# A chain of four layers on one core: the products of layers 1 and 2 in another order, both batches' high weight blocks first, then both batches' low ones

## The chip, the cores and the metric

The kernel runs on one core of a Trainium2 chip. TensorE multiplies, VectorE (DVE in the profile) and ScalarE (ACT) do elementwise work, GpSimd (POOL) folds and issues some transfers, SyncE (SP) issues most transfers. The metric is the time of one execution on the device in microseconds; lower is better. Times shown are of the slowest core, and there is only one.

## The reference, cut to what matters

`x` has 8 batches of 256 tokens by 1024 features. Four layers follow one another, each with a residual:

```python
x = x + L0(x)     # x W^T, plus a gated mixture of 8 rank-16 experts
x = x + L1(x)     # x W^T + b + coeff[b] * (x @ (2*mask[b] - 1))
x = x + L2(x)     # x @ weight[id[b]]^T
x = x + L3(x)     # (x @ B[id[b]]^T) @ A[id[b]]^T
```

In layer 1 the product's matrix is W^T plus a scaled mask of signs, another one for each batch; in layer 2 it is one of 8 weights, chosen for each batch by its id. So in layers 1 and 2 every batch has a 1024 by 1024 matrix of its own. Inputs are in float32.

## The kernel before, in words

**Precision by parts.** A float32 matrix is split into a high part ([...]`whi` for weights) and a low part (the rest, `wlo`). A product is high times high, plus high times low, plus low times high. Activations of layers 1 and 2 are kept in tiles `hl`, with the high and the low part of a batch's 256 tokens side by side, 512 columns. So a *unit*, which is one block m of 128 output features for one batch, takes eight wide products (a block of `whi` against 512 columns, one for each 128 input features k) and eight narrow ones (a block of `wlo` against the 256 high columns). Both kinds go into the same bank of PSUM; the evacuation adds its two halves. `two` writes these sixteen products: the loop at L529 with the wide ones at L531, the loop at L538 with the narrow ones at L540. Between the two loops it runs `mid`, pieces of other layers' work handed in by `main`; `early` comes after the second wide product. `late` stays empty.

**Batches and groups.** A pair q (0 to 3) is two batches, j = 0 and 1. Two pairs make a group g. Layer 0 is computed for a group at a time, in 16 slots s; then for each of its pairs come layer 1 and layer 2, each 16 units u, in the order m outside, j inside (in the last pair the last six units of layer 2 go by j outside). So even u is batch j = 0 of a block m and odd u is batch j = 1 of the same block.

**Joint units.** `main(n)` does one unit. In layer 1 for m < 7, and in layer 2 (in the last pair for u < 10), the two units of a block are *joint*: they share a PSUM tile of two banks (`ps`, two such tiles alternate), and both are evacuated at once after the odd one. The other units have a tile each.

**The order of each slot.** There is no scheduler: `unit_slot(n)` writes out what each engine does, and every engine keeps that order. It issues the load of the unit nine ahead, stores finished outputs, evacuates what the slots before have finished (ScalarE copies one half, VectorE adds the other: `c<-po` or `sum<-po`), casts the high part of the unit four ahead (`highs`, ScalarE, L288), adds W to a scaled mask (`merge_add`, VectorE; the W tile has two buffers), subtracts for the low parts (`lows`, VectorE, `wlo`), and then calls `main`. Low parts are made up to unit `f + LO_AHEAD + 1 - lag`, with LO_AHEAD = 3 and a lag of 1, more in the five slots of `LAGS` (L31) around the step from layer 1 to layer 2. There are five buffers of `whi` and four of `wlo`, and nine of raw weights or masks. A transfer that fills a raw buffer waits until the subtraction has read what was in it.

**Work put between.** In layer 2 of q = 1 and q = 3 the middle pieces are layer 3 of the pair before: `proj_pair` at u = 1 (L442), `rank_pair` at u = 3 (L453, L454), and at u = 5, 6, 7 and 8 `fill(2)`, which twice calls `finish`: two narrow products (L470) into a PSUM bank of its own, and an addition of it to the output rows on VectorE (`c<-pf`). Of the two `finish` in a fill the first takes bank 2 and the second bank 3, each time, and there is one buffer of each. In q = 1 the router's products of the next group stand at u = 13 (L308) and transposes of their result at u = 14 (L319). In q = 3, u = 9 has projections of the last two batches (L489), and others follow from u = 13 on.

Of the kernel before, what the change touches and what calls it, by code (L numbers as in the profile page):

```python
# [17 lines left out]
T = 256  # L18
N = 2 * T
K = 8  # L20
# [14 lines left out]
def kernel(ctx: ExitStack, tc: tile.TileContext, x, lang, coeff, ids,  # L35
# [28 lines left out]
    mm = nc.tensor.matmul  # L64
    copy = nc.scalar.copy

    def tt(o, a, b, op):
        nc.vector.tensor_tensor(o, a, b, op)  # L68
# [142 lines left out]
    def by_dma(q, m):  # L211
        return q % 2 == 0 and 2 * m < ADDED
# [20 lines left out]
    def fold_block(t, eng=None):  # L233

        (eng or nc.gpsimd).tensor_tensor(t, t, ident, ALU.add)  # L235
# [24 lines left out]
    def merge_add(n):  # L260
        _, q, m, j = items[n]
        s = f32(raws[n])
        if by_dma(q, m):
            fold_block(s[:, m, :])
            nc.gpsimd.dma_start(s, w1[m], accum_op=ALU.add)
            return
        if j == 0:
            fold_block(w1raw[q, m][:, m, :])
        tt(s, s, w1raw[q, m], ALU.add)
# [31 lines left out]
    def logits(p):  # L301


        g, j = p // 2, 1 - p % 2
        pl = bank(j, f"pl{p}")
        for k in range(K):
            c = 32 * (k % 4)
            mm(pl[c:c + 32, :], wrs[:, k, :], X[g][:, j, k, :], start=(k < 4), stop=(k >= 4))  # L308

        def leave():  # L310
            lgs[p] = gp.tile([P, N], F32, tag="lg", name=f"lg{p}", bufs=3)
            copy(lgs[p], pl)
        return leave

    def by_token(p):
        pts[p] = bank(1 - p % 2, f"pt{p}")
        lg = lgs.pop(p)
        for n in range(4):
            nc.tensor.transpose(pts[p][:, n * P:(n + 1) * P], lg[:, n * P:(n + 1) * P], ident)  # L319
# [114 lines left out]
    def proj_pair(q, n):  # L434


        pb = bank(n, f"pb{q}")
        for j in range(2):
            b = 2 * q + j
            for k in range(K):  # L440
                c = 32 * (k % 4)
                mm(pb[c:c + 32, j * T:(j + 1) * T], l3b[b][:, k, :], xts[b][:, k, :],  # L442
                   start=(k < 4), stop=(k >= 4))
        hi = gp.tile([P, N], FR, tag="lg", name=f"pbhi{q}", bufs=3)
        lo = gp.tile([P, N], FR, tag="lg", name=f"pblo{q}", bufs=3)
        copy(hi, pb)
        tt(lo, pb, f32(hi), ALU.subtract)
        prs[q] = hi, lo

    def rank_pair(q, n, banks):  # L450
        hi, lo = prs.pop(q)
        pr = bank(n, f"pr{q}")
        mm(pr[:96], sel3, hi, start=True, stop=False)  # L453
        mm(pr[:96], sel3, lo, start=False, stop=True)  # L454
        rt = l3p.tile([96, N], FR, tag="rt", name=f"rt{q}", bufs=1)
        copy(rt, pr[:96])
        tt(rt[32:64, :], pr[32:64, :], f32(rt[32:64, :]), ALU.subtract)
        for j in range(2):
            for m in range(0, K, 2):
                fillers.append(lambda b=2 * q + j, m=m, n=banks[m // 2 % 2]: finish(  # L460
                    b, m, rt[:, (b % 2) * T:(b % 2 + 1) * T], n))
# [14 lines left out]
    def fill(n=1):  # L476
        for _ in range(min(n, len(fillers))):
            fillers.pop(0)()
# [40 lines left out]
    def rank(b):  # L519
        sums.pop(b)()  # L520
        rt = third(b)
        for m in range(0, K, 2):
            fillers.append(lambda m=m: finish(b, m, rt, (0, 2)[m // 2 % 2]))


    def two(po, hi, lo, xhl, j, early=(), mid=(), late=()):


        for k in range(K):  # L529
            c = slice(k * P, (k + 1) * P)  # L530
            mm(po, hi[:, c], xhl[:, k, j].rearrange("p h t -> p (h t)"), start=(k == 0),  # L531
               stop=False)
            if k == 1:
                for f in early:
                    f()
        for f in mid:
            f()
        for k in range(K):  # L538
            c = slice(k * P, (k + 1) * P)
            mm(po[:, :T], lo[:, c], xhl[:, k, j, 0, :], start=False, stop=(k == K - 1))  # L540
        for f in late:
            f()

    def three(po, hi, lo, xhl, j):
        for k in range(K):
            c = slice(k * P, (k + 1) * P)
            for h in range(2):
                mm(po, hi[:, c], xhl[:, k, j, h, :], start=(k + h == 0), stop=False)  # L548
        for k in range(K):
            c = slice(k * P, (k + 1) * P)  # L550
            mm(po, lo[:, c], xhl[:, k, j, 0, :], start=False, stop=(k == K - 1))
# [45 lines left out]
    def link(*args, **kw):  # L597

        mm(*args, skip_group_check=True, **kw)  # L599
# [263 lines left out]

    pos_tile = {}

    def main(n):

        kind, q, m, j = slots[n]
        u = (pos[slots[n]]) % 16
        f = first[n]  # L870
        hi, lo = his.pop(f), los.pop(f)
        early, mid, late = [], [], []
        last = n == len(slots) - 1

        end = q == 3 and kind == "L2"
        joint = u < 10 if end else (m < K - 1 or kind == "L2")
        h = u % 2 if joint else 0
        if h == 0:
            pos_tile[0] = ps.tile([P, 2, N], F32, tag="mm", name=f"po{n}")
        po = pos_tile[0][:, h, :]  # L880
        xh = hls[kind, q]
        if kind == "L1":
            if u == 0:
                hls["L2", q] = hl_tile(GX[q // 2], f"hl2_{q}")
        else:
            if u == 0:
                i = 2 - 2 * (q % 2)
                xt2 = G[q // 2][:, i:i + 2].rearrange(
                    "p j a (b t) -> p j (a b) t", b=2)
                xts[q, 2] = xt2  # L890
                xts[2 * q], xts[2 * q + 1] = xt2[:, 0], xt2[:, 1]
            if q % 2:
                if u == 1:
                    mid = [lambda: proj_pair(q - 1, 2)]
                if u == 3:
                    mid = [lambda: rank_pair(q - 1, 3, (2, 3))]
                if 5 <= u < 9:
                    mid = [lambda: fill(2)]
            if q == 1:
                if u == 13:  # L900
                    mid = [lambda: [leave() for leave in [logits(p) for p in (2, 3)]]]
                if u == 14:
                    mid = [lambda: [by_token(p) for p in (2, 3)]]
            if q == 3:
                b = NB - 1
                if u == 9:
                    mid = [lambda: proj(b - 1, 0, 0), lambda: proj(b, 0, 1)]
                if u == 13:
                    mid = [lambda: proj(b - 1, 1, 0)]
                if u == 14:  # L910
                    early = [lambda: rank(b - 1)]
                    mid = [lambda: fill(2)]
        if last:

            po = po[:, :T]
            three(po, hi, lo, xh, j)
        else:
            two(po, hi, lo, xh, j, early=early, mid=mid, late=late)
        if joint and u % 2 == 0:
            return  # L920
        js = slice(0, 2) if joint else slice(j, j + 1)
        po = pos_tile[0] if joint else pos_tile[0][:, :1, :]
        if last:
            po = po[:, :, :T]
        if kind == "L1":
            x2 = hls["L2", q][:, m, js]
            done.append((po, b1_sb[:, m:m + 1], None, x2[:, :, 0, :], x2[:, :, 1, :]))
        else:
            done.append((po, None, xts[q, 2][:, js, m, :], None, None))
# [36 lines left out]
    def unit_slot(n):  # L966
        kind, q, m, j = slots[n]
        f = first[n]
        i = pos[slots[n]]
        g, ahead = divmod(i + LOAD_AHEAD, 64)  # L970
        if g == q // 2:
            load_unit(i + LOAD_AHEAD)
        elif g == 1 and ahead < 8:
            name, h = W0_LOADS[ahead]
            alloc_w0(1, name, h)
            load_w0(1, name, h)
        store()
        lag = LAGS.get((kind, m, j), 1)
        bulk = [lambda u=u: merge_add(u) for u in merges.get(n, [])]
        bulk.append(lambda: lows(f + LO_AHEAD + 1 - lag))  # L980

        urgent = (m, kind) in ((0, "L1"), (0, "L2"), (K - 1, "L2"))
        if (kind, m, j) == ("L1", 0, 0):
            l0_evacuate(q // 2, 16) if q % 2 == 0 else None
        evacuate(bulk.pop(0) if not urgent else None)
        highs(f + HI_AHEAD)
        for work in bulk:
            work()
        fold(f + HI_AHEAD + 1)
        fold(f + HI_AHEAD + 2)  # L990
        side(n)
        main(n)
        for u in merges.get(n + 1, []):
            merge_scale(u)
# [29 lines left out]
    for h in range(2):  # L1024
        for k in range(2):
            m = 2 * h + k
# [111 lines left out]
```

## Time and profile before

| | |
|---|---|
| median of 3 runs | 603.26 us (603.24 to 603.83) |
| the profiled execution's own time | 603.36 us |
| its span in the profile | 601.0 us |
| TensorE busy | 593.1 us, 99% of the span |
| weight loads busy | 499.1 us, 83% |
| VectorE busy | 474.2 us, 79% |
| ScalarE busy | 385.7 us, 64% |
| GpSimd busy | 135.2 us, 23% |
| granted TensorE clock | 0.997 |
| wide products, L531 | 1016 |
| narrow products, L540 | 1016 |

The profile is of one execution. Line numbers such as L531 are of the kernel before. A row of groups gives the line, engine, operation, output and inputs by the program's names, shapes, how many there were, then busy time in us, the mean of one in ns, the idle time of the engine before them and what ended it. A row of the order in time gives the start in us from the span's beginning, the time from the first start to the last end, engine, line, names and how many stand in a row, with the idle time before and its releaser in brackets. A row of the chain gives the start, the share of time in us, engine, line and how many. Products overlap one another in TensorE's pipeline, so what a product costs in a row of products is the distance from its start to the next start.

### The profile page before, as it was taken

The numbers are of one execution on the slowest core, as the hardware profiler recorded it, in microseconds if no ns is written. First come the engines' busy times: TensorE is split into PE (matmuls) and PEld (weight loads), VectorE is DVE, ScalarE is ACT, GpSimd is POOL, SyncE is SP. The second block draws the span as 40 slices with busy tenths as digits, with TensorE's granted clock in tenths as the row PEclk, the third lists the DMA queues.
The fourth block names the chain that finished last, engine by engine and source line by source line (L and its number), as shares of the span: only waits on it lengthen the run. The fifth ranks groups of instructions, "written<-read, shape, count | busy, mean of one in ns | idle before, by whom it ended". The sixth has DMA issues, their size and how long they took to land.

```text
span 601.0 us, 8936 instructions
## 1 busy us (share of the span) xinstructions
PE 593.1 (99%) x3240; PEld 499.1 (83%) x3240; DVE 474.2 (79%) x561; ACT 385.7 (64%) x457; POOL 135.2 (23%) x174
## 2 busy tenths in 40 slices
PE   9999999999999999999999999999999999999995
PEld 7777888888888888888778888888888888888884
DVE  5579688899699899586755796789978999977853
ACT  5667566687669787543553874568866788864431
POOL 0322250114241213122110234111423111521000
PEclk9999999999999999999999999999999999999998
DMA  8987894667685877599940799836767686847504
GB/s 283 343 199 165 191 233 137 200 235 267 208 278 188 283 257 265 209 347 322 268 70 24 156 249 233 250 105 210 285 204 255 205 294 228 301 154 232 190 1 140
DMA packets 39533, 130.22 MB, mean 217 GB/s; under 512 B 4802, under 2 KB 6466, under 8 KB 38722
## 3 DMA queue, kind: packets, MB, share of 16 engines
q1 hardware_dynamic: 34594, 112.36, 53.7%
q0 software_dynamic: 4608, 16.78, 15.3%
q8 instruction: 25, 0.41, 0.3%
q10 hardware_dynamic: 288, 0.52, 0.3%
q14 instruction: 18, 0.15, 0.1%
HBM read 121.25 MB, written 8.39 MB: 216 GB/s over the span
## 4 chain that ended last, share of the span: by engine, by line
PE 97%; ACT 1%; DVE 1%; issue 0%; DVEq 0%; POOL 0%; POOLq 0%; ACTq 0%
PE po L531 39%; PE mm L599 30%; PE po L540 20%; PE pl L308 1%; PE pf L470 1%; PE pb L442 1%; PE ph L626 1%; PE ph L627 1%; PE ph L625 1%; PE warm L1010 1%; PE pb L489 0%; ACT x L698 0%; DVE c L68 0%; PE po L548 0%; PE pg L392 0%
## 5 line engine op out<-in xcount | busy, mean ns | idle before, releaser
L531 PE MATMUL po<-hl,whi 128*128 128x512 f32 x1016 | 254.5, 392 | 0.0
L531 PEld LDWEIGHTS po<-hl,whi 128*128 128x128 f32 x1016 | 182.8, 189 | 32.7
L68 DVE TENSOR_TENSOR wlo<-raw,whi 128x1024 fp32r<-128x1024 f32 x128 | 160.8, 1266 | 1.3 <-issue 1.2
L540 PEld LDWEIGHTS po<-hl,wlo 128*128 128x128 f32 x1016 | 137.6, 190 | 11.3 <-issue 1.6
L288 ACT CAST whi<-raw 128x1024 fp32r<-128x1024 f32 x128 | 133.7, 1048 | 18.0 <-PE mm L599 8.4
L540 PE MATMUL po<-hl,wlo 128*128 128x256 f32 x1016 | 142.4, 283 | 0.0
L599 PE MATMUL mm<-whi,whi 128*128 128x512 f32 x224 | 88.6, 396 | 0.0
L599 PE MATMUL mm<-wlo,whi 128*128 128x512 f32 x224 | 87.9, 392 | 0.0
L235 POOL TENSOR_TENSOR raw<-raw,ident 128x128 f32<-128x128 f32 x72 | 60.5, 843 | 115.6 <-DMA raw<-in_w 100.8
L257 ACT ACTIVATE raw<-raw,negc,c 128x1024 f32<-128x1024 int32 x64 | 79.5, 1242 | 3.9 <-DMA raw<-in_mask 3.9
L599 PE MATMUL mm<-whi,wlo 128*128 128x512 f32 x224 | 70.8, 391 | 0.0
L68 DVE TENSOR_TENSOR raw<-raw,w 128x1024 f32<-128x1024 f32 x56 | 68.8, 1228 | 1.4 <-issue 1.4
L235 POOL TENSOR_TENSOR w<-w,ident 128x128 f32<-128x128 f32 x28 | 31.1, 1112 | 167.7 <-DMA w<-in_w 120.1
L68 DVE TENSOR_TENSOR wlo<-x,whi 128x1024 fp32r<-128x1024 f32 (+1 forms) x38 | 44.8, 1187 | 11.6 <-issue 6.8
L599 PEld LDWEIGHTS mm<-whi,whi 128*128 128x128 f32 x224 | 42.2, 189 | 11.1 <-issue 1.1
L288 ACT CAST whi<-A 128x1024 fp32r<-128x1024 f32 x26 | 27.3, 1051 | 36.2 <-PE mm L599 24.5
L599 PEld LDWEIGHTS mm<-whi,wlo 128*128 128x128 f32 x224 | 42.2, 188 | 9.2 <-DVE wlo L68 0.2
L599 PEld LDWEIGHTS mm<-wlo,whi 128*128 128x128 f32 x224 | 42.2, 188 | 8.6
L572 ACT COPY c<-po 128x512 f32<-128x512 f32 (+1 forms) x34 | 18.7, 551 | 45.9 <-PE po L540 45.9
L575 ACT ACTIVATE sum<-po,b_sb 128x512 f32<-128x512 f32 (+1 forms) x36 | 23.1, 640 | 31.0 <-PE po L540 30.9
L288 ACT CAST whi<-x 128x1024 fp32r<-128x1024 f32 x34 | 35.2, 1048 | 11.1 <-PE mm L599 8.8
L68 DVE TENSOR_TENSOR c<-mm,c 128x1024 f32<-128x1024 f32 x20 | 24.4, 1221 | 21.8 <-PE mm L599 21.8
(126 smaller groups left out, 523.8 us busy)
## 6 DMA issues: line engine op xcount, KB each, us to landing
raw<-in_mask SPq DMA_DIRECT2D x64, 512.0 KB, 5.4
raw<-in_w SPq DMA_DIRECT2D x64, 512.0 KB, 4.8
w<-in_w SPq DMA_DIRECT2D x28, 512.0 KB, 3.4
out<-c SPq DMA_DIRECT2D x29, 256.0 KB, 3.2
A<-in_w SPq DMA_DIRECT2D x14, 512.0 KB, 8.6
x<-in_x SPq DMA_DIRECT2D x6, 1024.0 KB, 7.8
A<-in_w POOLq DMA_DIRECT2D x12, 512.0 KB, 8.5
x<-in_x POOLq DMA_DIRECT2D x12, 512.0 KB, 8.5
```

The source lines that it names most:

```text
L68: nc.vector.tensor_tensor(o, a, b, op)
L235: (eng or nc.gpsimd).tensor_tensor(t, t, ident, ALU.add)
L257: nc.scalar.activation(f32(raws[n]), raws[n], AF.Identity, bias=negc[:, b:b + 1], scale=c2[:, b:b + 1])
L288: copy(prep_hi(i), flat(source(i)))
L308: mm(pl[c:c + 32, :], wrs[:, k, :], X[g][:, j, k, :], start=(k < 4), stop=(k >= 4))
L442: mm(pb[c:c + 32, j * T:(j + 1) * T], l3b[b][:, k, :], xts[b][:, k, :], start=(k < 4), stop=(k >= 4))
L470: mm(po[:, i * T:(i + 1) * T], at[:, (m + i) * P:(m + i + 1) * P], rt, start=True, stop=True)
L531: mm(po, hi[:, c], xhl[:, k, j].rearrange("p h t -> p (h t)"), start=(k == 0), stop=False)
L540: mm(po[:, :T], lo[:, c], xhl[:, k, j, 0, :], start=False, stop=(k == K - 1))
L572: copy(xs, po[:, :, T:])
L575: nc.scalar.activation(xs, po[:, :, T:], AF.Identity, bias=b1c)
L599: mm(*args, skip_group_check=True, **kw)
```

## The change

The function `two` is taken apart into `high_run` (the wide products, with `early` and `mid`) and `low_run` (the narrow ones). `main` does the high run at once and puts the low run into a list. For the even unit of a joint pair it then returns; for every other unit the list is emptied before the evacuation is noted. So a joint pair gives: high run of j = 0, high run of j = 1, low run of j = 0, low run of j = 1. A middle piece stays behind the high run of its own unit: that of an odd unit then stands ahead of both low runs, that of an even unit between the two high runs.

As the low run of an even unit is written only in the slot of the odd one, its `wlo` buffer is given back there, and the lag is raised to 2 in the odd slots of joint pairs: an odd slot makes no new low part, and an even one makes two. The products are the same in number and in operands; `link` is the matmul call without the check for interleaved groups.

```diff
-    def two(po, hi, lo, xhl, j, early=(), mid=(), late=()):
+    def high_run(po, hi, xhl, j, early=(), mid=()):
         for k in range(K):
             c = slice(k * P, (k + 1) * P)
-            mm(po, hi[:, c], xhl[:, k, j].rearrange("p h t -> p (h t)"), start=(k == 0),
-               stop=False)
+            link(po, hi[:, c], xhl[:, k, j].rearrange("p h t -> p (h t)"), start=(k == 0),
+                 stop=False)
             if k == 1:
                 for f in early:
                     f()
         for f in mid:
             f()
+
+    def low_run(po, lo, xhl, j, late=()):
         for k in range(K):
             c = slice(k * P, (k + 1) * P)
-            mm(po[:, :T], lo[:, c], xhl[:, k, j, 0, :], start=False, stop=(k == K - 1))
+            link(po[:, :T], lo[:, c], xhl[:, k, j, 0, :], start=False, stop=(k == K - 1))
         for f in late:
             f()
...
+    low_runs = []
+
+    def is_joint(kind, q, m, u):
+        return u < 10 if (q == 3 and kind == "L2") else (m < K - 1 or kind == "L2")
...
-        end = q == 3 and kind == "L2"
-        joint = u < 10 if end else (m < K - 1 or kind == "L2")
+        joint = is_joint(kind, q, m, u)
...
         else:
-            two(po, hi, lo, xh, j, early=early, mid=mid, late=late)
+            high_run(po, hi, xh, j, early=early, mid=mid)
+            low_runs.append(lambda: low_run(po, lo, xh, j, late=late))
         if joint and u % 2 == 0:
             return
+        while low_runs:
+            low_runs.pop(0)()
...
         lag = LAGS.get((kind, m, j), 1)
+        if i % 2 and is_joint(kind, q, m, i % 16):
+            lag = max(lag, 2)
```

## The prediction

> **What bounds the kernel now.** I read the page first: the engines' shares, then the chain that ended last, then the costliest groups. The chain names the bound:
>
> ```profile
> PE 97%; ACT 1%; DVE 1%; issue 0%; DVEq 0%; POOL 0%; POOLq 0%; ACTq 0%
> ```
> ```profile
> L531 PE MATMUL po<-hl,whi 128*128 128x512 f32 x1016 | 254.5, 392 | 0.0
> L68 DVE TENSOR_TENSOR wlo<-raw,whi 128x1024 fp32r<-128x1024 f32 x128 | 160.8, 1266 | 1.3 <-issue 1.2
> L540 PE MATMUL po<-hl,wlo 128*128 128x256 f32 x1016 | 142.4, 283 | 0.0
> ```
>
> TensorE carries 97% of the chain and is idle 0.0 us before the 1016 wide products (L531) and the 1016 narrow ones (L540). So no wait in layers 1 and 2 is there to be removed; the change can win only in the spacing of products, and can lose by any new wait of TensorE. For the spacing I read the starts on TensorE, where layer 1 of the third group of batches begins:
>
> ```profile
> 404.36 1.98 PE L531 MATMUL po<-hl,whi 128*128 128x512 f32 x8
> 406.18 1.11 PE L540 MATMUL po<-hl,wlo 128*128 128x256 f32 x8
> 407.13 2.00 PE L531 MATMUL po<-hl,whi 128*128 128x512 f32 x8
> 408.97 1.12 PE L540 MATMUL po<-hl,wlo 128*128 128x256 f32 x8
> 409.92 2.00 PE L531 MATMUL po<-hl,whi 128*128 128x512 f32 x8
> ```
>
> Read differences of starts, not durations (they overlap). The first high run follows wide products of layer 0 and takes 1.82 us; the next, after eight narrow ones, takes 1.84. A low run takes 0.95 us, a unit 2.79. In nanoseconds the same starts give 1814 against 1840, and the eight steps after a low run read 233, 236, 228, 232, 231, 227, 227, 225: the first wide products after narrow ones are slow, then the pace is 227. The chain shows that pace in a layer-0 stretch:
>
> ```profile
> 310.56 2.72 PE mm L599 x12
> ```
>
> 2.72/12 = 0.227 us, so 8 take 1.814.
>
> **The skill.** "TensorE: Matmul & The Clock Gate", section "LDWEIGHTS (loading the stationary operand)", prices a load of 128 columns at columns/1.2 ns, 107 ns; section "Back-to-back issue gap" prices a warm matmul at columns/2.4 + 2.5 ns: 109 for 256 columns, 216 for 512. So a narrow product is about as long as its weight load[...]. The trace agrees in kind and is slower: 120 ns narrow, 227 wide. "PSUM — Partial Sum Buffer", section "Engine vs sequencer instructions", says VectorE and ScalarE run strictly in order: an added subtraction ahead of an evacuation delays it. The trace shows no overtaking.
>
> **Part 1: the runs.** A joint pair now is high, low, high, low: 2 x (1840 + 953) = 5586 ns. After it is high 1840, high 1814, low 953, low after a low run 960 (no fast first step: 268.41 to 269.37 below is such a run after narrow products, 0.96). Sum 5567; gain 19 ns. Joint pairs: 7 in each of four layer-1 stages (28), 8 in each layer 2 of q = 0, 1, 2 and 5 in q = 3 (29): 57. In five of them something stands between the two high runs, because the middle work of an even unit is still done after its own high run: the fills (pf, L470) of u = 6 and 8 in q = 1 and in q = 3, and the transposes of u = 14 in q = 1. With narrow products between them, the second high run starts slow again: no gain there. 52 x 19 = 1.0 us gained. The transposes hand over to a wide run instead of a low one; nearest row: the wide product after a projection took 338 ns instead of 233, against 201 instead of 113 for the low one, so about 0.03 us lost, once.
>
> **Part 2: the low subtractions in pairs.** The lag moves the subtraction (wlo) of an even unit to the next even slot: VectorE does nothing of it in odd slots, and two in a row in even ones. Count and work unchanged; cost nothing where the operand stays early. In the trace wlo ends 4.8 us or more before its use in the steady parts; an even unit's comes 2.79 later, its use 1.84 later: still about 4. At the entries to the layers (3.7 us to layer 1, down to 2.2 to layer 2) the order of the subtractions stays as it was. Cover gone, it would cost 2.79 - 1.84 = 0.95 us for each late pair. Partial sums are evacuated no later: the addition stands ahead of the two subtractions. No DMA changes its place in SP's or POOL's queue; an odd unit's reload waits on the even subtraction and may issue 2.7 us later, covered by 10 us or more for layer-2 weights and by the wait for the W buffer for most masks.
>
> **Part 3: the fills collide.** This is where a cover is gone. Layer 2 of q = 1:
>
> ```profile
> 266.09 2.00 PE L531 MATMUL po<-hl,whi 128*128 128x512 f32 x8
> 267.93 0.64 PE L470 MATMUL pf<-rt,a 96*128 96x256 f32 x4
> 268.41 1.12 PE L540 MATMUL po<-hl,wlo 128*128 128x256 f32 x8
> 269.37 2.00 PE L531 MATMUL po<-hl,whi 128*128 128x512 f32 x8
> 271.21 0.64 PE L470 MATMUL pf<-rt,a 96*128 96x256 f32 x4
> ```
> ```profile
> 266.91 0.69 DVE L68 TENSOR_TENSOR c<-po,c 128x512 f32<-128x512 f32 x1 [0.53 <-ACT c L572]
> 267.51 1.22 DVE L68 TENSOR_TENSOR wlo<-raw,whi 128x1024 fp32r<-128x1024 f32 x1
> 268.65 1.28 DVE L68 TENSOR_TENSOR c<-pf,c 128x512 f32<-128x512 f32 x2
> ```
>
> The fill of u = 6 starts at 267.93 into banks 2 and 3; VectorE adds them out (c<-pf, two of 0.68, 0.60 apart), free at 269.33 and 269.93. The fill of u = 7 wants bank 2 at 271.21 and bank 3 at 271.45. Cover now: 1.88 and 1.52 us. The change puts the low run of u = 6 behind u = 7's fill: the two fills come nearer by 0.96. And slot 6 now holds two subtractions ahead of the additions instead of one: VectorE later by 1.13 (267.51 to 268.65). Cover after: 1.88 - 2.09 = -0.21 and 1.52 - 2.09 = -0.57. TensorE waits until both banks are free, 0.57 in all, and 0.055 from VectorE's end to TensorE's start (as for L1071 near the end: 593.809 to 593.864): 0.62 us. In q = 3 the same instructions stand at 560.02 and 563.30, additions at 560.74, the same cover: another 0.62. Together 1.25 us lost. From u = 5 to 6 an odd unit's fill is followed by two low runs and a high run (0.48 + 1.92 + 1.84 us), and from u = 7 to 8 likewise: no wait. All work behind the wait on TensorE, so everything, moves by it.
>
> **Part 4: layer 2 needs its input sooner.** The second unit of layer 2 reads the last block of layer 1 (m = 7, second batch) in its eighth product. The first entry:
>
> ```profile
> 156.93 2.00 PE L531 MATMUL po<-hl,whi 128*128 128x512 f32 x8
> 158.77 1.12 PE L540 MATMUL po<-hl,wlo 128*128 128x256 f32 x8
> 159.73 2.00 PE L531 MATMUL po<-hl,whi 128*128 128x512 f32 x8
> ```
> ```profile
> 159.18 0.69 DVE L68 TENSOR_TENSOR hl<-sum,hl 128x256 fp32r<-128x256 f32 x1
> ```
>
> That block is written at 159.87. After the change the eighth product wants it at 156.93 + 1.84 + 7 x 0.227 = 160.36: 0.5 us cover. At the other entries the block is done at 248.98, 451.76 and 541.07 against 249.75, 452.46 and 541.84: 0.7 to 0.8. No cost; each us of delay beyond costs one.
>
> **Sum.** -1.00 + 0.03 + 1.25 = +0.28 us on the profiled execution's 603.36, its 601.0 span and 2.4 around it, which stay. Against the median of the runs shown (603.26): 603.5.
>
> **Rivals.** *A, as above, 603.5: 64%.*
>
> *B, the fills don't wait*, because VectorE reaches the additions sooner than counted; for it: only 0.57 has to be made good; against it: the start of VectorE's slot is tied to TensorE's end of the pair, and subtraction and additions had no idle time between them. Gain alone: 603.26 - 0.97 = 602.3, on the edge of what can be told: 13%, a third of it beyond the edge.
>
> *C, long wide runs go faster than 227 ns*, towards the skill's 216: 8 x 11 ns x 52 = 4.6 us, 598.9 and with the fills' wait some 600. Against it: the 240 wide products of layer 0 in a row from 349 on take 55.06 us, 229 each. 8%, for this or any other gain not seen.
>
> *D, slower: late masks.* In layer 1 of q = 1 and 3, masks for u = 4 to 9 land only 0.02 to 0.8 us before ScalarE scales them (0.0 to 0.4 at u = 4 to 6). With VectorE's merges in odd slots standing behind two subtractions (+1.13 us), the loop mask, scale, merge, W buffer free, next load may slip each round. High weights there are ready at 202.29 for 210.01 (q = 1, u = 3), 7.7 us, of which the change takes 0.95. Until the slip passes 6.8 us nothing shows; from there each us costs one, twice. It ends above 0.2% from about 0.5 us past it in each stage; at 8 us: 603.5 + 2 x 1.2 = 605.9. Against it: merges that free the W buffer stand mostly in even slots, ahead of the subtractions. With the entries of part 4: 15%.
>
> That the change doesn't do what it says is excluded: in the built order of TensorE two runs of x8 wide stand before two of x8 narrow.
>
> **Range and chances.** From B's 602.3 with the runs' scatter (0.6) to A plus one more wait of the fills' size: 602.1 to 604.4. It leaves out C and most of D, some 20%. A alone: 603.1 to 603.9. 0.2%, 1.2 us, is about what a measurement of this kernel can tell from no change. Faster by more: C and a third of B, 12%; slower: D, 15%; within: 73%.
>
> **What would show it.** In layer 2 of q = 1 and 3, TensorE idle about 0.2 and 0.4 us before two pf products of u = 7, ended by VectorE's c<-pf; starts of a pair 5.57 apart instead of 5.59; low runs of sixteen in 1.91; the first L2 pair without idle time. No wait at u = 7 makes it B; idle time before whi or hl products makes it D.

## The result, and the profile after

The changed kernel takes 605.83 us (median of 7, 604.55 to 606.73) against 603.26 us of the kernel before: ratio 1.0036, 95% interval 1.0022 to 1.0049. It is slower, by about 2.2 us by this ratio and 2.6 us between the medians, where 603.5 was predicted. The profiled execution took 605.46 us, its span is 603.2 us (before: 603.36 and 601.0).

The page of the changed kernel, the rows that answer to those shown of the kernel before: the chain by engine, then the costliest groups.

```profile
PE 89%; DMA 5%; DVE 2%; ACT 1%; issue 1%; SPq 0%; DVEq 0%; ACTq 0%
...
L602 PE MATMUL po<-hl,whi 128*128 128x512 f32 x1016 | 244.8, 391 | 0.0
...
L68 DVE TENSOR_TENSOR wlo<-raw,whi 128x1024 fp32r<-128x1024 f32 x128 | 158.4, 1276 | 0.0
```

The products of layers 1 and 2 themselves still wait for nothing (idle 0.0 before the wide ones, and 0.0 before the narrow ones too). TensorE's share of the chain has fallen from 97% to 89%, but most of that misleads: the pieces of DMA (5%, 28 us) all lie before 42 us, where the change has done nothing yet and layer 1 even began sooner than in the kernel before. What is new further on are short pieces of other engines; of the chain in order of time:

```profile
266.03 2.62 DVE wlo L68 x2
268.65 1.21 DVE c L68 x2
...
295.64 0.61 ACT laghi L654
```

The first two come once more at 560.74. From layer 1 on, the list of TensorE's waits names two that the kernel before did not have:

```profile
PE pt L319 <- ACT lg L312: 1.7, 1, 1.7
...
PE pf L470 <- DVE c L68: 0.8, 2, 0.4
```

**The runs did what was counted.** TensorE in order of time, at the start of layer 2 of q = 0:

```profile
155.78 3.82 PE L602 MATMUL po<-hl,whi 128*128 128x512 f32 x16
159.43 2.08 PE L602 MATMUL po<-hl,wlo 128*128 128x256 f32 x16
161.34 3.82 PE L602 MATMUL po<-hl,whi 128*128 128x512 f32 x16
```

Sixteen wide products last 3.65 us (155.78 to 159.43; in nanoseconds 3654 = 1840 + 1814), sixteen narrow ones 1.91, a pair 5.57. The first two rows are the first pair of layer 2, which follows layer 1 without idle time; the third row begins the second pair.

**The fills wait.** TensorE, then VectorE, at u = 5 to 8 of layer 2 of q = 1:

```profile
264.60 2.00 PE L602 MATMUL po<-hl,whi 128*128 128x512 f32 x8
...
266.92 2.00 PE L602 MATMUL po<-hl,whi 128*128 128x512 f32 x8
269.31 1.10 PE L470 MATMUL pf<-rt,a 96*128 96x256 f32 x4 [0.38 <-DVE c L68]
...
272.15 2.00 PE L602 MATMUL po<-hl,whi 128*128 128x512 f32 x8
```
```profile
266.03 2.62 DVE L68 TENSOR_TENSOR wlo<-raw,whi 128x1024 fp32r<-128x1024 f32 x2
268.57 2.57 DVE L68 TENSOR_TENSOR c<-pf,c 128x512 f32<-128x512 f32 x4
```

From the start of u = 6 to that of u = 8 it is now 7.55 us (264.60 to 272.15), 6.56 before (266.09 to 272.65). The fill of u = 7 could start at 268.76 (266.92 + 1.84) and starts at 269.31, and its four products then take 0.94 us instead of 0.48. In q = 3 the same stretch takes 7.56 us. So 1.00 us is lost twice; 0.62 each was predicted.

**The transposes wait, which was not predicted.** TensorE at u = 14 of q = 1 in the changed kernel, and ScalarE at that time:

```profile
296.79 1.14 PE L319 MATMUL pt<-ident,lg 128*128 128x128 f32 x8 [1.67 <-ACT lg L312]
```
```profile
294.17 0.62 ACT L654 CAST laghi<-c 128x512 fp32r<-128x512 f32 x1 [2.44 <-DMA c<-in_la]
...
296.16 1.06 ACT L312 COPY lg<-pl 128x512 f32<-128x512 f32 x2
```

ScalarE keeps the order written in the kernel. Ahead of its two copies of the router's logits (`lg`, L312: the results of the router's products), which the transposes read, stand two casts (`laghi`, L654; the second starts at 295.64) of the `la` block, experts' weights for the next group's layer 0. That block is one transfer, `in_la`, issued by SP at u = 10. In the kernel before, ScalarE reads:

```profile
292.05 0.62 ACT L651 CAST laghi<-c 128x512 fp32r<-128x512 f32 x1 [1.46 <-DMA c<-in_la]
...
294.04 1.06 ACT L312 COPY lg<-pl 128x512 f32<-128x512 f32 x2
```

Already there ScalarE waited for the block, and the first of the two copies was done at 294.62; the transposes started at 295.50, as soon as TensorE was free. With some 0.05 us from a copy's end to a transpose (296.73 to 296.79 after the change) the cover, the time by which the logits could come later without a wait, was 0.83 us. After the change the block lands 2.12 us later (294.14 against 292.03), and TensorE is there 0.54 us sooner (294.96): 2.12 + 0.54 - 0.83 = 1.83 us, and the transposes do start at 296.79, 1.83 us after TensorE could have begun them. The list shows 1.67 of it as idle time.

**Why the block lands late.** SP's queue, before and after:

```profile
266.85 0.41 SPq L203 DMA_DIRECT2D A<-in_w  x1
269.36 0.93 SPq L474 DMA_DIRECT2D out<-c  x2
270.34 0.45 SPq L209 DMA_DIRECT2D x<-in_x  x1
```
```profile
264.40 0.41 SPq L203 DMA_DIRECT2D A<-in_w  x1
269.28 0.93 SPq L474 DMA_DIRECT2D out<-c  x2
270.26 0.46 SPq L209 DMA_DIRECT2D x<-in_x  x1
```

The order in the queue is the same. But the stores of u = 6 (L474) wait on VectorE's additions c<-pf, and these now stand behind two subtractions instead of one; and the loads of the next group (A, x) stand behind the stores. Between this A load and the x load there are 5.9 us instead of 3.5. The page "DMA: Bandwidth & Descriptors" of the Trainium skill, section "Anatomy of one DMA — SWDGE (gpsimd) path", a section on transfers issued by GpSimd, says that DMA engines don't wait on semaphores, that the issuing sequencer does, ahead of dispatch. The trace shows the same for SP: from 264 to 284 us its stores wait up to 4.4 us for VectorE's additions, and the loads behind them are not issued. A long wait alone is not the harm: the kernel before has one of 5.3 us, which ends at 265.81, but ahead of it the queue had been filled by loads (x at 258.50, another at 259.44), and the transfer engines were 94% busy from 262 to 266. In the changed kernel, ahead of the wait that ends at 269.28, only one load was issued after that of 261.27, the A load at 264.40; the transfer engines run dry and move nothing at all from 269 to 270. In the table of stretches (busy us of each engine, then clock, share of the transfer engines, GB/s), from 266 to 270 us, before and after:

```profile
266.00:270.00 4.00, 4.00 (x26) 3.58 (x25) 3.47 (x6) 2.59 (x3) 1.22 (x1) 1.00 0.82 280
```
```profile
266.00:270.00 4.00, 3.52 (x18) 2.56 (x16) 4.00 (x6) 1.39 (x2) 1.49 (x3) 1.00 0.48 176
```

The engines are full from 278 us on. From 262 to 282 us (five stretches of 4 us, the sum of GB/s times 4) 6.70 MB were moved before and 6.27 MB after. This difference, 0.43 MB, is not all arrears: at 262 us the changed kernel was 0.43 MB ahead (62.12 MB since the start against 61.69). It loses that lead here, and at 282 us it is 0.10 MB behind (69.33 against 69.43 MB), an estimated 0.4 us at the 270 GB/s or so that the engines moved while the block was under way. How 2.1 us at the landing come of it is taken up below, under "All profiles together".

**The sum on the profiled executions.** Runs -1.0 (counted, not measured), fills +0.99 and +1.00, transposes +1.92 (from the high run of u = 14 to layer 0: 8.39 against 6.47 us), a projection's wait in layer 0 (L442) +0.17: +3.1. Layer 1 began 1.02 us sooner in this execution (111.25 against 112.27), in code that the change does not touch; over the profiles below that start lies between 111.5 and 112.6. That leaves 2.1, and the two own times differ by 2.10.

The theory of two waits, then: the fills cost 2.0 us through PSUM banks; and late additions cost up to 2 us through stores, loads, the `la` block (also called the router's block below), ScalarE and the transposes. The rivals: the transposes wait only because of the fills' wait; the late block is an accident of one execution; the loss lies in layer 1 (late masks, rival D).

### The profile page after: what moved, and what is told of

The parts are those of the page before. It is cut to its first block, busy times and chain, and to the rows that moved or that the text cites. A ratio compares the mean times of both kernels' runs of the same rounds, so it can differ in the third digit from the quotient of the medians.

```text
span 603.2 us, 8923 instructions
## 1 busy us (share of the span) xinstructions
PE 592.5 (98%) x3240; PEld 498.6 (83%) x3240; DVE 474.5 (79%) x561; ACT 385.4 (64%) x457; POOL 124.7 (21%) x174
## 3 DMA queue, kind: packets, MB, share of 16 engines
HBM read 121.25 MB, written 8.39 MB: 215 GB/s over the span
## 4 chain that ended last, share of the span: by engine, by line
PE 89%; DMA 5%; DVE 2%; ACT 1%; issue 1%; SPq 0%; DVEq 0%; ACTq 0%
PE po L602 58%; PE mm L602 26%; DMA x<-in_x 3%; DMA A<-in_w 2%; DVE wlo L68 1%; PE pf L470 1%; PE pb L442 1%; DVE c L68 1%; PE ph L628 1%; PE ph L629 1%; PE ph L630 1%; PE pl L308 1%; ACT x L701 0%; PE pb L489 0%; PE po L551 0%
## 5 line engine op out<-in xcount | busy, mean ns | idle before, releaser
L602 PE MATMUL po<-hl,whi 128*128 128x512 f32 x1016 | 244.8, 391 | 0.0
L602 PEld LDWEIGHTS po<-hl,whi 128*128 128x128 f32 x1016 | 186.0, 188 | 35.6
L68 DVE TENSOR_TENSOR wlo<-raw,whi 128x1024 fp32r<-128x1024 f32 x128 | 158.4, 1276 | 0.0
L602 PEld LDWEIGHTS po<-hl,wlo 128*128 128x128 f32 x1016 | 130.4, 191 | 7.2 <-issue 1.6
L602 PE MATMUL po<-hl,wlo 128*128 128x256 f32 x1016 | 133.3, 283 | 0.0
L235 POOL TENSOR_TENSOR raw<-raw,ident 128x128 f32<-128x128 f32 x72 | 53.2, 740 | 120.9 <-DMA raw<-in_w 97.3
L235 POOL TENSOR_TENSOR w<-w,ident 128x128 f32<-128x128 f32 x28 | 27.3, 976 | 172.1 <-DMA w<-in_w 131.6
L68 DVE TENSOR_TENSOR c<-po,c 128x512 f32<-128x512 f32 (+1 forms) x38 | 24.1, 641 | 28.1 <-ACT c L575 27.0
```

## The experiments

All are measured beside the kernel before on one chip for each group of four. The edits are to the changed kernel where nothing else is said.

### Each wait removed alone, both removed, and the stores moved

**Four banks.** The fills of successive units take banks 0 and 1, then 2 and 3, and so on.

```diff
-                    mid = [lambda: rank_pair(q - 1, 3, (2, 3))]
+                    mid = [lambda: rank_pair(q - 1, 3, (0, 1, 2, 3))]
...
-                fillers.append(lambda b=2 * q + j, m=m, n=banks[m // 2 % 2]: finish(
+                fillers.append(lambda b=2 * q + j, m=m, n=banks[m // 2 % len(banks)]: finish(
```

> The changed kernel, with the eight fills of layer 3 going round four PSUM banks (0, 1, 2, 3) instead of two. Theory F (two waits for a bank, 1.0 us each by the profile after): no idle time of TensorE at u = 7 in q = 1 and 3, a pair with two fills back at 6.56 us from 7.55, 2.0 us less: 605.8 - 2.0 = 603.8. The additions and stores of the fills don't come sooner, so the wait of the transposes for lg stays at 1 to 3 us. Rival R (the loss is the paired low subtractions on VectorE, whatever the bank): the idle time moves to other products and the time stays at 605 to 606.

Measured: 604.21 us (602.83 to 606.57, 22 runs) beside 603.56 of before; ratio 1.0016, 1.0006 to 1.0025. The profile is of one of its slower executions, 605.86 us. The fills don't wait any more (u = 6 to 8 in 6.56 us); the transposes do, and longer, because TensorE is there sooner: 2.1 us in the list of waits. The block landed at 294.11. So the second wait does not come from the first.

**The casts behind the logits.** ScalarE's casts of the `la` block, and with them VectorE's two subtractions for its low part, move from u = 12 and 13 to u = 15 and into layer 0, behind the copies `lg`.

```diff
-            if u in (12, 13):
-                la_parts(1, 4 * (u - 12), 4 * (u - 12) + 4)
             if u == 15:
+                la_parts(1, 0, 4)
                 router([2, 3])
...
+            at(1, lambda: la_parts(1, 4, 8))
             at(2, lambda: expand(p0))
```

> The changed kernel, with the two splits of the experts' weights of group 1 (laghi, laglo) moved on ScalarE and VectorE from u = 12 and 13 of q = 1 to u = 15 and to slot 1 of layer 0. Theory L (the copies lg of the logits stand on ScalarE behind a cast that waits for in_la's landing, and the transposes wait for lg): the transposes no longer wait, the projections after them lose their 0.17 us too: 605.8 - 1.9 = 603.9; waits at the fills stay, 1.0 us each. Rival (lg is late for another reason): the transposes still wait 1 to 2 us, 605.5 to 606.

Measured: 603.99 us (603.35 to 605.15, 20 runs); ratio 1.0006, 0.9999 to 1.0013. The block lands as late as ever (294.41), and the transposes don't wait for it; the fills' wait stays.

**Both.**

> Both edits together. If the fills (2.0 us) and the transposes (1.9 us) are the whole loss, what is left is the gain of the runs: 603.3 - 1.0 = 602.3, and no idle time of TensorE between 112 and 585 us above 0.15. Rival R: 604 or more.

Measured: 602.09 us (601.41 to 603.13, 21 runs); ratio 0.998, 0.9973 to 0.9986: faster than the kernel before. Set against it on the same chip, the fills' wait is worth 603.99 - 602.09 = 1.9 us and the transposes' 604.21 - 602.09 = 2.1 us. That is 4.0 us together, a little more than the 3.4 us between this ratio and the changed kernel's 1.0036: each was taken with the other wait gone, and where the fills don't wait the transposes wait longer.

**The stores behind.** In each slot of layers 1 and 2 SP issues the stores after the slot's other loads instead of ahead of them; nothing else is moved.

```diff
-        store()
         lag = LAGS.get((kind, m, j), 1)
...
         side(n)
+        store()
         main(n)
```

> The changed kernel, with the stores of finished rows issued after the slot's other loads instead of before them. Theory S (in_la lands late because loads of x and W stand on SP behind stores that wait for the additions of u = 6, and the DMA engines run dry for 1 to 1.5 us just before 270 us): the DMA share in the 4 us before 270 goes from 0.48 to 0.8 or more, in_la lands at least 1 us sooner than 294.1, and the transposes wait 0 to 0.9 us instead of 1.7; the time falls by 1 us, to 604.8. Rival (the landing's lateness comes from slow packets later, between 281 and 294): in_la lands within 0.5 us of 294, the wait stays above 1.2, 605.5 to 606.

Measured: 604.03 us (603.29 to 605.02, 20 runs); ratio 1.0008, 1.0001 to 1.0015. SP's queue now reads

```profile
265.71 1.14 SPq L209 DMA_DIRECT2D x<-in_x  x1
270.13 0.94 SPq L474 DMA_DIRECT2D out<-c  x2
```

The x load is issued at 265.71, ahead of the stores that wait, instead of behind them at 270.26; the transfer engines are 93% busy from 266 to 270, and the block lands at 289.00. The transposes don't wait, although ScalarE's order is that of the changed kernel. This is the link that the trace alone could not show: with the stores out of the loads' way the block is no longer late. The time fell further than expected (604.8). The kernel before was not run with its stores moved, so what this edit would give by itself is not known.

### The change taken apart

**The changed kernel again**, on another chip.

> The changed kernel itself once more, beside the following three on one chip, so that each can be set against it. The theory of two waits (the fills' second pair waits 2.0 us for its banks, and the transposes wait some 1.9 us for the logits, because the last load of the router's block comes late) expects 605 to 606 again, 1.0025 to 1.0045 of the kernel before, with both waits in its profile. If the first measurement was of its chip alone: within 0.2% of before.

Measured: 605.15 us (604.59 to 605.87, 6 runs) beside 603.38; ratio 1.0031, 1.0019 to 1.0043. The loss is not of one chip. The profiled execution was the fastest of the six; its fills wait as before, its transposes only 0.3 us, with the block at 293.29. So the size of the second wait differs from one execution to the next.

**The pairing alone**: the kernel before, its products in the old order, with two subtractions in each even slot.

```diff
         lag = LAGS.get((kind, m, j), 1)
+        u = i % 16
+        if u % 2 and (u < 10 if (q == 3 and kind == "L2") else (m < K - 1 or kind == "L2")):
+            lag = max(lag, 2)
```

> The kernel before with the second edit alone: the low subtractions come in pairs in even slots, TensorE's runs stay in their old order. If the pairing by itself makes the fills' additions, and so the stores, late enough to dry the loads, the router's block lands near 294 us as after the change, the transposes wait 1 to 2 us and the time is 604.5 to 605.5. If it takes both edits (additions 1.4 us later and TensorE's runs 1 us sooner), the block lands between 292 and 294, the fills don't wait (cover 1.5 us less 1.4), and the time is within 0.6 us of before, 603.0 to 604.2. Nothing is to be gained here: the narrow runs stay between the wide ones.

Measured: 605.79 us (604.52 to 607.70, 6 runs); ratio 1.0048, 1.0032 to 1.0065. The edit that was costed at nothing costs 2.4 us by itself, no less than the whole change beside it (1.8 us), and a little more than the expected 605.5 at most. No fill waits. A row of VectorE, then two of SP's queue:

```profile
270.07 1.28 DVE L68 TENSOR_TENSOR c<-pf,c 128x512 f32<-128x512 f32 x2
```
```profile
270.79 0.93 SPq L474 DMA_DIRECT2D out<-c  x2
271.77 0.45 SPq L209 DMA_DIRECT2D x<-in_x  x1
```

Additions, stores and the x load are all 1.4 us later than in the kernel before (270.07 for 268.65, 270.79 for 269.36, 271.77 for 270.34). Of this, 0.3 us is a later start of layer 1 in this execution (TensorE's high run of u = 6 starts at 266.38 for 266.09); the rest, 1.1 us, is the second subtraction. In this execution, again the fastest of its kernel, the block landed at 293.66 and the transposes waited 0.4 us.

**The order alone**: the change without its lag.

```diff
-        if i % 2 and is_joint(kind, q, m, i % 16):
-            lag = max(lag, 2)
```

> The changed kernel without its second edit: TensorE's runs in the new order, one low subtraction in each slot as before. The fills of u = 6 are then added out some 1.4 us sooner, behind one subtraction, so the second pair of fills doesn't wait (2.0 us less than the changed kernel); stores of even units leave sooner too, so the router's block should land at 292 to 293.5 us and the transposes wait under 1 us. On the other side the subtraction of an odd slot must wait for its buffer until the even unit's low run is done, which now comes after the odd high run; the trace gives it 3 us or more until its use, so that should cost nothing. Expected 602.3 to 603.3. If the wait for the buffer reaches TensorE, the profile shows waits of po for wlo and the time is 604 or more.

Measured: 605.19 us (604.65 to 606.71, 7 runs); ratio 1.0032, 1.0020 to 1.0043. The expectation failed. Of VectorE's rows:

```profile
264.81 1.23 DVE L68 TENSOR_TENSOR wlo<-raw,whi 128x1024 fp32r<-128x1024 f32 x1 [2.29 <-issue]
265.95 1.28 DVE L68 TENSOR_TENSOR c<-pf,c 128x512 f32<-128x512 f32 x2
...
268.88 1.28 DVE L68 TENSOR_TENSOR c<-pf,c 128x512 f32<-128x512 f32 x2
```

VectorE stands still for 2.29 us ahead of the odd slot's subtraction. The trace names no releaser, but it starts 0.26 us after the even unit's low run is over (263.59 + 0.96), and the next one, at 271.78, does so too (270.56 + 0.96): that fits a wait for its buffer, which the low run gives back. The expectation asked only when that low part is needed, not what is queued behind it. Behind it stand the additions of u = 5, the evacuation, and then those of u = 6 (268.88). The fill of u = 7 starts in time but takes 0.4 us longer in each of q = 1 and 3 (0.89 for 0.48), the transposes wait 0.7, a projection in layer 0 (L442) 0.9. The block landed at 293.54. Either edit alone holds VectorE's additions back, in different ways, with the same end.

**Layer 2 of q = 1 and 3 as before**, both edits kept elsewhere (44 pairs).

```diff
+        if kind == "L2" and q % 2 and low_runs:
+            low_runs.pop(0)()
         if joint and u % 2 == 0:
             return
...
-        if i % 2 and is_joint(kind, q, m, i % 16):
+        if i % 2 and is_joint(kind, q, m, i % 16) and not (kind == "L2" and q % 2):
```

> The changed kernel with both edits kept in layer 1 and in layer 2 of the even groups (28 + 16 = 44 pairs), and undone in layer 2 of the odd groups, where fills, stores and the router stand. The theory of two waits expects neither of them, the spacing's gain of 44 x 19 ns = 0.84 us and nothing else: 0.6 to 1.1 us below before, ratio 0.9982 to 0.999. If part of the loss lies in layer 1 (late masks) or in the even groups, the time stays at or above before.

Measured: 603.06 us (602.00 to 605.23, 14 runs); ratio 0.9999, 0.9988 to 1.001. The time lies above the expected range; the gain can't be told from nothing. But no loss against the kernel before is left that can be measured (its interval ends at 0.1%), so the 2 us don't lie in layer 1 or the even groups: rival D falls. In the profile (602.59 us) the gain is there: from layer 1's first product to the last product 481.85 us against 482.53, and no wait of fills or transposes. But TensorE comes to the transposes at 294.96 and the first copy is done at 294.72: 0.18 us of cover is left, since the block lands as before (292.13). Whether its five executions of 604.0 us or more are those in which the block is later still was not seen.

### What the pairing and the gain are worth without the late block

**The pairing alone, casts behind the logits; and the kernel before with the casts moved.** The edits are those shown above.

> The pairing of the low subtractions alone (as in the run of the second edit alone, which took 2.4 us more than before, with fills that do not wait), and in it ScalarE's casts of the router's block moved behind its copies of the logits. If the pairing costs its 2.4 us through that one chain (additions, stores, loads, the router's block, casts, logits, transposes), all of it goes: within 0.15% of before, no wait of the transposes, though the block lands as late as it did. If part of the cost lies elsewhere (masks, reloads, the layers' entries), the time stays 0.2% or more above before.

> The kernel before with ScalarE's casts of the router's block moved behind its copies of the logits, and nothing else. Its transposes did not wait in the profile, but had only 0.4 us to spare: if the late block reaches them in some executions, the median falls by up to 0.4 us and the highest times come down; otherwise within 0.1% of before. The difference between this kernel and the next is the change's own gain once its two waits are gone: 1.0 us by the count of pairs.

Measured: 603.22 us (602.30 to 604.84, 21 runs), ratio 0.9992, 0.9984 to 1.0; and 603.29 us (602.66 to 604.56, 18 runs), ratio 0.9989, 0.9982 to 0.9997; beside 603.7 of before. The two are level, so within the 0.1% that can be told here all that the pairing costs goes through this one chain, although its block still lands at 294.55. In the first, ScalarE copies the logits from 292.98 on and casts the block from 296.31. The 0.4 us that the kernel before gains by the moved casts is what the last expectation allowed for a wait in some executions; the profiled one had none, so this stays open. (The 0.4 us to spare in that expectation was counted at the second copy; the transposes start when the first is done, with 0.83.)

**The changed kernel with both waits removed, once more; and with four banks and the stores behind.**

> The changed kernel with both waits removed (second pair of fills in banks of its own, casts behind the logits), once more beside the others: 0.9972 to 0.9986 of before as the first time, that is 0.8 to 1.7 us less, and about 1.0 us less than the kernel before with the casts moved. If it is level with that one, the gain was the casts' and not the change's.

> The changed kernel with the fills in four banks, and, in place of the moved casts, the stores put behind the following unit's other work, so that the loads aren't held up on SP. The block should land by 290 us, neither fills nor transposes should wait, and the time should be that of the version with the moved casts within 0.1%. If the stores' place matters only through the late block, the two are level; if it costs at the end of the kernel or elsewhere, this one is 0.3 us or more slower, as the version with moved stores and waiting fills was by 0.2 us against its 603.3 expected.

Measured: 602.01 us (601.45 to 603.22, 13 runs), ratio 0.9975, 0.9965 to 0.9985; and 601.77 us (601.49 to 602.44, 5 runs), ratio 0.9959, 0.9945 to 0.9973. Against the kernel before with the casts moved the change gains 603.29 - 602.01 = 1.3 us; 1.0 was counted from the pairs, and the intervals don't part the two. In the profiles, from layer 1's first product to the last product, it is 0.9 us: 482.53 in the kernel before, 481.6 to 481.7 in the three with both waits removed. The version with four banks and the stores behind leaves ScalarE as it was, and is the fastest here, level with the other. In its profile neither fills nor transposes wait (u = 6 to 8 in 6.56 us), and the block lands at 290.04.

**All profiles together.** What was moved from 262 to 282 us (worked out as above), what was moved from the start to 282 us (the sizes of all packets in the trace), and when the block was issued and landed:

| kernel | MB, 262 to 282 | MB by 282 | block issued, us | landed, us |
|---|---|---|---|---|
| four banks, stores behind | 6.88 | 69.81 | 281.1 | 290.0 |
| stores behind | 6.75 | 69.76 | 280.6 | 289.0 |
| before | 6.70 | 69.43 | 282.6 | 292.0 |
| before, casts behind | 6.70 | 69.47 | 281.9 | 290.2 |
| layer 2 of q = 1, 3 as before | 6.60 | 69.51 | 281.7 | 292.1 |
| order alone | 6.35 | 69.29 | 282.4 | 293.5 |
| changed | 6.27 | 69.33 | 281.2 | 294.1 |
| pairing alone | 6.26 | 69.00 | 283.2 | 293.7 |
| pairing alone, casts behind | 6.25 | 69.17 | 281.9 | 294.6 |
| changed, casts behind | 6.23 | 69.26 | 282.0 | 294.4 |
| four banks, casts behind (twice) | 6.13, 6.08 | 69.35, 69.30 | 281.9, 281.4 | 293.9, 294.0 |
| four banks | 6.06 | 69.27 | 282.0 | 294.1 |
| changed, again | 6.04 | 69.29 | 281.6 | 293.3 |

The moment of issue does not decide the landing: the changed kernel issues the block 1.4 us sooner than the kernel before and gets it 2.1 us later. The first two columns both part the kernels into the same two classes: with 6.6 MB or more, or 69.43 MB or more since the start, the block lands by 292.1; with less it doesn't land before 293.3. But since the start the two classes lie only 0.08 MB apart, so being behind at 282 us goes with a late landing and does not account for its size. More of it shows between issue and landing: there the engines moved 3.46 MB in the changed kernel and 2.55 MB in the kernel before, at 267 and 271 GB/s. In the changed kernel a load that GpSimd issued after the block (A, 512 KB) had landed before it (293.56 for 294.14), in the kernel before it came after it (294.06 for 292.03). Why more of the later loads get ahead of the block's last packet was not pursued. Within each class the landings scatter by 1 to 3 us, 1.8 us of it between the kernel before and the same with its casts behind.

## Why the prediction was wrong

**Part 1, the runs: right.** 5.57 us for a pair, sixteen narrow in 1.91, no gain at the pairs with fills between. The gain is real, 0.9 us in the profiles and 1.3 between medians against the 1.0 counted, once nothing eats it.

**Part 2, the pairing: this step failed.** "Cost nothing where the operand stays early" looked at the readers of the low parts alone. About these it was right: past the entries, no low part in the changed kernel is ready less than 3.6 us before its use. "No DMA changes its place in SP's or POOL's queue" was true and beside the point: the place stayed, the time did not. Part 3 itself counted VectorE's additions 1.13 us later; the stores behind those additions, and the loads behind those stores, were not followed. The term for this path in the sum was nothing. Nor was the other end of the chain looked up: in the trace before, ScalarE's copies of the logits had 0.83 us of cover behind a transfer that was already being waited for. Alone, this edit measured 2.4 us.

**Part 3, the fills: right in mechanism and place, short in size**, 2.0 us instead of 1.25. Two terms of the sum were too small. The two subtractions took 2.54 us to the additions (266.03 to 268.57) and not 2.27 (2 x 1.133): the second took 1.49 us, while GpSimd folded. "SBUF — State Buffer" of the Trainium skill, section "Who interferes with whom", says that a VectorE tensor_tensor with both inputs in SBUF contends with GpSimd's reads. The trace agrees for some of the overlaps: in the kernel before, 25 of the 128 such subtractions took over 1.3 us (mean 1.47), each of them with a fold of GpSimd (L235) at the same time; three more such took 1.26 to 1.29, and all others at most 1.23. And starting again costs more than the 0.055 of latency: the four fill products took steps of 223, 374, 222 and 119 ns where 120 each is usual. The first product after a wait takes 0.10 more; in the step of 374 lies the wait for the second bank, so of the two only the 0.10 behind that wait is added. 0.62 + 0.27 for the subtractions + 0.10 = 0.99, against 1.00 measured.

**Part 4, the entries: right**, no idle time at any step from layer 1 to layer 2.

**Rivals.** B's 602.3 is nearly what the kernel gives when the fills don't wait and the block is out of the way, but its condition did not hold. C did not show: sixteen wide products go at 228 ns each (its sum, 603.26 - 4.6, is 598.7 and not 598.9, which changes nothing). D had the right sign and, at an assumed 8 us of slip, nearly the right time (605.9), by luck: no high run of layer 1 waits. The range's upper end allowed one more wait of the fills' size, predicted at 0.62; the one that came was worth 2.1 us between the medians, three times as much.

## What to carry to other kernels

When an instruction moves on an engine, follow everything that stands behind it on that engine, and everything behind those instructions' results in other queues: a store that waits for them holds back each load behind it. What shows it is the share of the transfer engines in that stretch, not the order in the queue and not the length of the wait alone. When bytes are compared between two kernels in a fixed stretch of time, count also how far ahead each one was at its start. Look also at transfers that an engine already waits for in the trace (here 1.46 us on ScalarE), ask what stands behind that wait and how much cover it has, since a faster TensorE takes from the same cover. In this kernel, issuing the stores behind the loads that follow them took the second wait away without a touch on ScalarE; it is worth trying where no buffer has to come free by the store.

## What the runs showed of the hardware that was not expected

- A VectorE subtraction of 128x1024 takes 1.22 us. In the kernel before, 64 of the 128 overlap a fold of GpSimd. Where the subtraction began first (30), none took over 1.23 us. Where the fold began first (34), 25 took over 1.3 us, 1.47 on average. So a fold slows a subtraction here only if it is under way when the subtraction begins.
- The first narrow product after a wait of TensorE takes 0.22 us instead of 0.12: at both waits of the fill of u = 7, in q = 1 and in q = 3.
- The `la` block of 512 KB, issued into full queues, landed after 8.4 us (stores behind), 9.4 (before) and 13.0 (changed); in these times the engines moved 2.57, 2.55 and 3.46 MB, five to seven times the block itself. Over all fourteen profiles 8.3 to 13.0 us go with 2.4 to 3.5 MB.
